# Two attention layers on one core: the values of the first block loaded early, activations in six tiles, relative terms in three

## The chip, the cores and the metric

One core of a Trainium2 chip runs the whole program. The time is device microseconds from start to end of one execution; the comparison is between medians of several executions. A profile is one further execution with the hardware profiler on; it has its own time, and a span from its first to its last instruction that is a little shorter.

Engines are named as the profile names them: PE multiplies matrices, PEld loads its stationary operand, DVE and ACT work on tensors, POOL and SP issue DMAs here (POOL nearly all stores, SP nearly all loads). In the profile SPq and POOLq are the places from which SP and POOL issue DMAs.

## The reference

Two layers of the same shape on an image of 48 x 48 tokens with 768 channels: group norm, attention with 12 heads and a relative-position term for rows and one for columns, an output projection, and the residual. Cut to what matters:

```python
h = group_norm(x, 32)                       # over tokens and 24 channels
qkv = h @ qkv_w + qkv_b                     # layer 0 adds low-rank terms to q and v
attn = einsum('bqc,bkc->bqk', q * scale, k)
rel_h = einsum('bhwc,hkc->bhwk', r_q, Rh)   # r_q is q as (head, 48, 48, 64)
rel_w = einsum('bhwc,wkc->bhwk', r_q, Rw)
attn = attn + rel_h[..., :, None] + rel_w[..., None, :]
x = x + (softmax(attn) @ v) @ proj_w + proj_b
```

In layer 1 the weights are transposed and q is scaled twice. There are 2304 queries and 2304 keys for each head, in float32.

## The kernel before

Activations lie transposed, channels on the partitions: `xT` holds six blocks of 384 tokens (NQB, QB) times six channel tiles of 128 (CT). In this version `xT` is one tile. It is filled once by transposes (`load_transposed`, L165), normalised in place (`normalise`, L246), and read by the projections.

A layer runs through these stages, PE in the order in which they stand:

1. **Projections of k and v** (`project_kv`, L474), by products of half blocks (`seven_products`, L429).
2. **Projection of q** (`project_q`, L599), in two halves of three head pairs. A half loops over the six token blocks b: three groups of q matmuls (L691), each read out by DVE (`x_q`, L697), then `store` (L616): the block is split into a high and a low part, by ACT (L384) and then DVE (L385), and both go to DRAM from POOL's queue (`f_q<-xs_q`, L626). Then ACT copies the block into `columns` (L702), and `rel_h` (L640) makes the row terms of the previous block one block late. After the sixth block comes `rel_w` (L661): 16 steps of six small matmuls each (psc, L633), each followed by a split of its result, ACT (`relw`, L387) and then DVE (L388). Only after the last step are the two parts of the column terms stored (`f_r<-relw`, L680), one DMA of 2592 KB for each part.
3. **Attention** (`attend_plain`, L852), a list of 30 blocks: for each of six head pairs, queries 0, 512, 1024, 1536 (512 each) and 2048 (256). k, v, q and the relative terms come back from DRAM scratch. In a block, 18 key tiles (NKT) of 128 keys go in batches of six: PE computes scores of six key tiles (8 matmuls q times k in two parts, and 2 matmuls that add the relative terms, L944), ACT takes the exponential, DVE sums, and then PE makes the products with v (`values`, L991) of the batch before. So PE's order is: scores 0 to 5, [values 12 to 17 of the block before], scores 6 to 11, values 0 to 5, scores 12 to 17, values 6 to 11, scores 0 to 5 of the next block, values 12 to 17. The sums of the exponentials are multiplied by ones (`denominators`, L1000, psum `ps_d`) right after values 16 (`kt == NKT - 2`), and `finish` (L1012) multiplies by the reciprocal (L1010) and stores.
4. **Output projection** (`out_project`, L1101), again by seven products of half blocks (`psy`, L1151), which loads the attention output back (`fetch_output`, L1089 and L1095) into tiles named in `first_out` (L1246) for its first pair of token blocks. In layer 0 these tiles are blocks 2 and 5 of the next layer's `xT`.

**How loads are cut.** `fetch_keys`, `fetch_queries` return a tile and a `step(g)`, g from 0 to 2; `fetched` runs step 0 of all its arguments, then step 1, then step 2. Group g of the keys is a third of the 2304 keys (768); key tiles 0 to 5 need group 0 of keys and of the relative terms, tiles 6 to 11 group 1, tiles 12 to 17 group 2. Group g of the relative terms is eight DMAs of 96 KB: rel_h (L925) and rel_w (L929) for two parts and two heads. The three groups lie in one tile `rel`. `fetch_values` issues one DMA of 1152 KB when it is called (L897), which for the first block is after all 6 loads of k, 2 of q and 24 of rel (L1026 and L1027).

**What sets the order.** A scheduler in the framework places instructions, with lists in places kept in program order (`in_order`, L158). [...] A new tile in a pool waits for every access to each whole tile whose space it takes. So one large tile comes free when its last reader is done. The program also holds a second, shifted version of attention for large inputs (`attend_plain` is the one that runs).

Of the kernel before, what the change touches and what calls it, by code (L numbers as in the profile page):

```python
# [18 lines left out]
P = 128  # L19
# [52 lines left out]
def compute(ctx: ExitStack, tc: tile.TileContext, x, layers, out, run, bad):  # L72
# [85 lines left out]
    def in_order(instruction):  # L158

        tc.keep_in_program_order(instruction)  # L160
# [4 lines left out]
    def load_transposed(xT, raw, res, weights, low_rank):  # L165


        with tc.tile_pool(name="ps_x", bufs=3, space=PSUM) as ps_x:
            loaded = [xT[:, b].rearrange("p t q -> p (t q)") for b in range(NQB)]
            loaded = [l.rearrange("p (j c) -> p j c", j=TPB) for l in loaded]  # L170
            for b in range(NQB):
                nc.sync.dma_start(loaded[b], x[ts(b, QB), :].rearrange("(j p) c -> p j c", p=P))
            weights.load(0)
            weights.begin()
            if not shifted:
                load_places()
            for b in range(NQB):
                if b == 2:
                    next(low_rank)
                for t in range(CT):  # L180
                    ps = ps_x.tile([P, QB], F32, tag="ps", name=f"psx_{b}_{t}")
                    for j in range(TPB):
                        in_order(nc.tensor.transpose(
                            ps[:, ts(j, P)], loaded[b][:, j, ts(t, P)], ident
                        ))
                    nc.scalar.copy(raw[b][:, t, :], ps)
                    nc.vector.bn_stats(stats[:, t, b, :], raw[b][:, t, :])

            weights.spread()
            for b in range(HB):  # L190
                for i in (b, b + HB):
                    in_order(nc.gpsimd.dma_start(res[i], raw[i]))

    def group_norm(xT, raw, gn, between, beside):
# [51 lines left out]
        def normalise(b):  # L246
            for t in range(CT):
                nc.vector.tensor_scalar(  # L248
                    xT[:, b, t, :], raw[b][:, t, :], mean[:, t : t + 1],
                    rstd[:, t : t + 1], ALU.subtract, ALU.mult,  # L250
                )
# [125 lines left out]
    def in_parts(hi, lo, x, scale=None, bias=None):  # L377


        if bias is not None:  # L380
            nc.scalar.activation(hi, x, AF.Identity, bias=bias)
            nc.vector.scalar_tensor_tensor(lo, x, bias, hi.bitcast(F32), ALU.add, ALU.subtract)
        elif scale is not None:
            nc.scalar.mul(hi, x, scale)  # L384
            nc.vector.scalar_tensor_tensor(lo, x, scale, hi.bitcast(F32), ALU.mult, ALU.subtract)  # L385
        else:
            nc.scalar.copy(hi, x)  # L387
            nc.vector.tensor_sub(lo, x, hi.bitcast(F32))  # L388
# [85 lines left out]
    def project_kv(ly, li, xT, kv, weights, first, normalise, PARTS, PART, kd, vd):  # L474


        with ExitStack() as es:
# [7 lines left out]
            def x_factors(b):  # L485
                for i in (b, b + HB):
                    normalise(i)
                blocks = {
                    f"{i + 1}{j + 1}": xT[:, b + j * HB, i * HP : (i + 1) * HP]
                    for i in range(2) for j in range(2)  # L490
                }
                t = kv.tile([P, 4, HP, QB], F32, tag=f"t{b}", name=f"xt_{b}")
                factors.append(sums_of_b(blocks, t))
# [105 lines left out]
    def project_q(ly, li, xT, weights, qd, rel_d):  # L599
# [4 lines left out]
        with ExitStack() as es:  # L604
# [55 lines left out]

            def rel_w(half, x):  # L661

# [3 lines left out]
                ]  # L666
                for l0 in range(0, HG, 3):
                    ps = ps_rel.tile(
                        [2 * HG, 3, HP, HG], F32, tag="rel", name=f"psc_{half}_{l0}"
# [12 lines left out]
            for half in range(2):  # L682
                w, _ = weights.take("q", half)
                columns = one.tile([P, HP, HG, HG], F32, tag="columns", name=f"columns_{half}")
                for b in range(NQB):
                    x = bp.tile([P, HP, QB], F32, tag="x", name=f"x_q_{half}_{b}")
                    for pr in range(HP):
                        pair = half * HP + pr
                        ps = ps_mm.tile([P, QB], F32, tag="mm", name=f"ps_q_{pair}_{b}")
                        for t in range(CT):  # L690
                            nc.tensor.matmul(  # L691
                                ps, lhsT=w[:, t, ts(pr, P)], rhs=xT[:, b, t, :],
                                start=(t == 0), stop=(t == CT - 1),
                            )
# [5 lines left out]
                        )  # L700
                    store(qd[half], b, x, f"xs_q_{half}_{b}", HD**-0.5)
                    nc.scalar.copy(  # L702
# [6 lines left out]
                while later:  # L709
                    later.pop()()  # L710
                rel_w(half, columns)

# [139 lines left out]
    def attend_plain(li, qd, kd, vd, rel_d, od, beside):  # L852
# [11 lines left out]
        with ExitStack() as es:  # L864
# [30 lines left out]
            def fetch_values(pair):  # L895
                v = sets[pair % 2].tile([P, NKT, P], F32, tag="v", name=f"v{li}_{pair}")
                nc.sync.dma_start(v, vd[:, ts(pair, P)].rearrange("(t p) d -> p t d", p=P))  # L897
                return v

            def fetch_queries(i, pair, at, n):  # L900
# [3 lines left out]
                into = sets[i % 2]  # L904
                rel = into.tile([P, NG, NG, QS], F32R, tag="rel", name=f"rel_{pair}_{at}")
                rel = rel[:, :, :, 0:n]
                q = [
                    into.tile([P, QS], F32R, tag=f"q{i}", name=f"q_{pair}_{at}_{i}")[:, 0:n]
                    for i in range(2)
                ]  # L910

                def step(g):
# [3 lines left out]
                    for i in range(2):  # L916
                        for r in range(2):
# [7 lines left out]
                            nc.sync.dma_start(  # L925
                                rel[row : row + KG, g].bitcast(F32),
                                rel_h[:, g : g + 1].to_broadcast((KG, NG, n)),
                            )
                            nc.sync.dma_start(  # L929
                                rel[row + KG : row + 2 * KG, g].bitcast(F32), rel_w  # L930
                            )
# [14 lines left out]
            class Block:  # L946


                def __init__(self, pair, at, n, keys, v, queries):
                    self.pair, self.at, self.n = pair, at, n  # L950
                    self.keys, self.v, self.queries = keys, v, queries
                    self.ps = self.sum = self.sums = self.first = self.rec = None

                def scores(self, kt):
# [5 lines left out]
                    steps = [(k, q) for k in keys for q in (hi, lo)]  # L960
                    steps.append((places[:, b % 2], rel[:, b // 2, c]))
                    for i, (k, q) in enumerate(steps):
# [62 lines left out]

            keys, queries = fetched(fetch_keys(0), fetch_queries(0, *blocks[0]))  # L1026
            v = fetch_values(0)  # L1027
            behind = []

            def catch_up():  # L1030

                for block, kt, pt in behind:
                    block.values(kt, pt)
                    if kt == NKT - 2:
                        block.denominators()
# [4 lines left out]
            for i, (pair, at, n) in enumerate(blocks):  # L1040
# [7 lines left out]
                if pair + 1 < CT and at == 2 * QS:  # L1048
                    next_v = fetch_values(pair + 1)
                for k0 in range(0, NKT, BATCH):  # L1050
# [50 lines left out]
    def out_project(ly, li, od, w, bt, first, res, xT, next_res, beside):  # L1101
# [3 lines left out]
        with ExitStack() as es:  # L1105
# [11 lines left out]
            for at, b in enumerate((1, 0, 2)):  # L1117
# [3 lines left out]
                if not last:  # L1121
                    y = [xT[:, i] for i in pair]
                elif at == 0:
# [60 lines left out]
    def begin(li, es):  # L1184
# [6 lines left out]
        weights.room(es)  # L1191
        xT = xp.tile([P, NQB, CT, QB], F32, tag="xT", name=f"xT{li}")
        return xT, gn, weights
# [3 lines left out]
    for li, ly in enumerate(layers):  # L1197
        last = li == len(layers) - 1
        with tc.tile_pool(name="p1_kv", bufs=1, **REUSE) as kv:
            raw = [xT[:, b] for b in range(NQB)]  # L1200
            low_rank = weights.low_rank(kv)
# [17 lines left out]
        with tc.tile_pool(name="p3_w", bufs=1, **REUSE) as p3:  # L1219
# [24 lines left out]
            else:  # L1244
                xT, gn, weights = begin(1, es)
                first_out = [xT[:, HB - 1], xT[:, NQB - 1]]  # L1246
                weights.begin()
# [72 lines left out]
```

## Time and profile before

| what | value |
|---|---|
| median of 3 runs | 3375.26 us (3374.58 to 3379.72) |
| profiled execution | 3375.62 us |
| its span | 3373.9 us |
| granted TensorE clock, mean | 0.985 |
| PE busy | 3263.2 us, 97% of the span |
| DVE busy | 2104.7 us, 62% |
| ACT busy | 1426.5 us, 42% |
| POOL busy | 387.3 us, 11% |
| DMA | 405.60 MB, mean 120 GB/s |

The profiled execution lies 0.4 us from the median, so that the working on its span can be set against the median as it is. The clock is the share of full speed that the throttle granted to TensorE. A row such as "x24 | 17.11 <-DMA v<-f_v" in the answers means 24 instructions merged, and in brackets the idle time of the engine just before, with what ended it. The positions of the stages, in us from the span's start: the q matmuls of layer 0 end at 483.3 and its attention runs from 504.0 to 1563.8; the same for layer 1 is 2129.9, and 2151.5 to 3215.9. The output projection of layer 0 begins at 1568.05.

### The profile page before, as it was taken

The numbers are of one execution on the slowest core, as the hardware profiler recorded it, in microseconds if no ns is written. First come the engines' busy times: TensorE is split into PE (matmuls) and PEld (weight loads), VectorE is DVE, ScalarE is ACT, GpSimd is POOL, SyncE is SP. The second block draws the span as 40 slices with busy tenths as digits, with TensorE's granted clock in tenths as the row PEclk, the third lists the DMA queues.
The fourth block names the chain that finished last, engine by engine and source line by source line (L and its number), as shares of the span: only waits on it lengthen the run. The fifth ranks groups of instructions, "written<-read, shape, count | busy, mean of one in ns | idle before, by whom it ended". The sixth has DMA issues, their size and how long they took to land. (4 is left out here: it accounts for less than half of the span.)

```text
span 3373.9 us, 50053 instructions
## 1 busy us (share of the span) xinstructions
PE 3263.2 (97%) x19708; PEld 2003.5 (59%) x19708; DVE 2104.7 (62%) x2275; ACT 1426.5 (42%) x1655; POOL 387.3 (11%) x719
## 2 busy tenths in 40 slices
PE   8999997999999999999989999799999999999997
PEld 5556664565666565655555566556565656665654
DVE  8432445777777677676774234477777777777753
ACT  3101444555555555553011024455555555555511
POOL 2144110000000000000012531000000000000000
PEclk9999998999999999999999999899999999999999
DMA  6333468453536353524234345753444453534241
GB/s 260 135 76 90 150 217 217 91 115 86 126 73 140 73 136 76 109 63 166 87 133 136 57 126 187 234 156 88 118 95 118 90 123 81 128 73 97 75 153 58
DMA packets 221202, 405.60 MB, mean 120 GB/s; under 512 B 41584, under 2 KB 109072, under 8 KB 217120
## 3 DMA queue, kind: packets, MB, share of 16 engines
q1 hardware_dynamic: 178656, 253.00, 30.6%
q0 software_dynamic: 42304, 149.31, 13.9%
q8 instruction: 159, 2.61, 0.3%
q14 instruction: 83, 0.68, 0.1%
HBM read 253.27 MB, written 148.89 MB: 119 GB/s over the span
## 5 line engine op out<-in xcount | busy, mean ns | idle before, releaser
L976 DVE TENSOR_TENSOR sum<-sum,pt 128x1024 f32<-128x1024 f32 (+1 forms) x960 | 1072.8, 1117 | 346.8 <-ACT pt L970 262.5
L970 ACT ACTIVATE pt<-ps_sc 128x1024 f32<-128x1024 f32 (+1 forms) x1080 | 992.0, 940 | 688.2 <-PE ps_sc L944 628.6
L944 PE MATMUL ps_sc<-q,k 64*128 64x512 f32 (+1 forms) x8640 | 1094.4, 372 | 9.5 <-ACT pt L970 8.1
L944 PEld LDWEIGHTS ps_sc<-q,k 64*128 64x128 f32 x8640 | 773.0, 185 | 272.7 <-issue 92.2
L944 PE MATMUL ps_ov<-pt,v 128*64 128x512 f32 (+1 forms) x4320 | 889.3, 556 | 31.5 <-DMA v<-f_v 31.5
L944 PEld LDWEIGHTS ps_ov<-pt,v 128*64 128x64 f32 x4320 | 294.7, 137 | 509.9 <-issue 439.4
L944 PE MATMUL ps_sc<-rel,places 64*128 64x512 f32 (+1 forms) x2160 | 409.9, 370 | 0.0
L1021 POOL DMA_DIRECT2D f_rec<-rec x120 | 58.5, 492 | 1993.3 <-DVE rec L1010 1993.1
L691 PE MATMUL ps_q<-xT,w_q 128*128 128x384 f32 x864 | 285.0, 489 | 0.7 <-DVE v L583 0.7
L1010 DVE RECIPROCAL rec<-ps_d 128x512 f32<-128x512 f32 (+1 forms) x60 | 182.2, 3037 | 100.4 <-PE ps_d L944 100.4
L691 PEld LDWEIGHTS ps_q<-xT,w_q 128*128 128x128 f32 x864 | 163.3, 191 | 110.8 <-issue 2.6
L944 PEld LDWEIGHTS ps_sc<-rel,places 64*128 64x128 f32 x2160 | 209.7, 185 | 28.8
L597 POOL DMA_DIRECT2D f_v<-v x288 | 137.9, 488 | 105.3 <-DVE v L583 94.0
L697 DVE TENSOR_SCALAR x_q<-ps_q,bt 128x384 f32<-128x384 f32 x72 | 44.4, 617 | 168.4 <-PE ps_q L691 168.4
L519 PE MATMUL ps_k<-xt,w_k 128*128 128x384 f32 x432 | 143.4, 487 | 3.6 <-DVE xt L423 2.6
L519 PE MATMUL ps_k<-xT,w_k 128*128 128x384 f32 x324 | 115.9, 511 | 4.7 <-DVE xT L248 4.6
L519 PEld LDWEIGHTS ps_k<-xt,w_k 128*128 128x128 f32 x432 | 81.5, 190 | 63.0 <-PE ps_k L519 3.0
L985 ACT CAST sum<-sum 128x1024 bf16<-128x1024 f32 (+1 forms) x60 | 57.6, 960 | 132.2 <-DVE sum L976 132.2
L384 ACT ACTIVATE xs_q<-x_q 128x1152 fp32r<-128x1152 f32 x24 | 27.9, 1163 | 196.6 <-DVE x_q L697 192.2
L988 DVE TENSOR_TENSOR sum<-sum,sum 128x1024 bf16<-128x1024 f32 (+1 forms) x60 | 67.1, 1119 | 61.6 <-ACT sum L987 61.6
L986 DVE TENSOR_TENSOR sum<-sum,sum 128x1024 f32<-128x1024 f32 (+1 forms) x60 | 67.1, 1119 | 61.6 <-ACT sum L985 61.6
L976 DVE TENSOR_TENSOR sum<-pt 128x1024 f32<-128x1024 f32 (+1 forms) x60 | 67.1, 1118 | 46.9 <-ACT pt L970 45.8
(186 smaller groups left out, 2426.0 us busy)
## 6 DMA issues: line engine op xcount, KB each, us to landing
rel<-f_r SPq DMA_DIRECT2D x1152, 96.0 KB, 4.1
f_k<-xs POOLq DMA_DIRECT2D x72, 384.0 KB, 2.9
f_q<-xs_q POOLq DMA_DIRECT2D x48, 576.0 KB, 3.8
k<-f_k SPq DMA_DIRECT2D x72, 384.0 KB, 5.5
q<-f_q SPq DMA_DIRECT2D x96, 256.0 KB, 3.0
f_r<-relh POOLq DMA_DIRECT2D x48, 432.0 KB, 5.0
f_r<-relw POOLq DMA_DIRECT2D x8, 2592.0 KB, 19.4
f_v<-v POOLq DMA_DIRECT2D x288, 48.0 KB, 2.0
```

The costliest lines, as they stand in the source:

```text
L519: nc.tensor.matmul(ps, lhsT=x, rhs=y, start=(t == 0), stop=(t == HP - 1))
L597: nc.gpsimd.dma_start(vd[to : to + KG, :], v[ts(r, KG), k])
L691: nc.tensor.matmul(ps, lhsT=w[:, t, ts(pr, P)], rhs=xT[:, b, t, :], start=(t == 0), stop=(t == CT - 1),)
L697: nc.vector.tensor_scalar(x[:, pr], ps, weights.bt[:, pair : pair + 1], ly.q_scale, ALU.add, ALU.mult,)
L944: in_order(nc.tensor.matmul(*args, **kwargs))
L970: nc.scalar.activation(pt, ps[:, :, 0 : self.n], AF.Exp)
L976: nc.vector.tensor_add(self.sum, self.first if kt == 1 else self.sum, pt)
L985: nc.scalar.copy(hi, self.sum)
L986: nc.vector.tensor_sub(self.sum, self.sum, hi)
L988: nc.vector.tensor_sub(lo, self.sum, mid)
L1010: nc.vector.reciprocal(self.rec, ps)
L1021: nc.gpsimd.dma_start(recs[li][2 * self.pair + r : 2 * self.pair + r + 1, to], self.rec[r * HD : r * HD + 1, :],)
```

## The change

Five edits, and what follows from them:

1. `xT` becomes six tiles, `xT[b]`, each with its own space and its own last reader. All uses are renamed.
2. `rel` becomes three tiles, `rel[g]`, allocated after the two q tiles.
3. `fetch_values` returns a tile and a `step`, with its one load in step 0. For the first block the tiles are allocated in the order keys, values, queries, and loaded in the order keys, queries, values: so v's load stands behind group 0 of k, q and rel, and ahead of group 1. With the new order of allocation v takes space of `x` instead of the weights' tables. For later pairs v is still asked for at query 1024.
4. In `project_q` the split and store of q of the last block of each half (`keep`) moves from before the columns copy into `rel_w`, after eight of its 16 steps. The two instructions of a scaled split are kept in program order.
5. In the last block of each layer (pair 5, queries 2048) `denominators` comes after values 17 instead of after values 16.

```diff
-            loaded = [xT[:, b].rearrange("p t q -> p (t q)") for b in range(NQB)]
+            loaded = [xT[b].rearrange("p t q -> p (t q)") for b in range(NQB)]
...
-            nc.scalar.mul(hi, x, scale)
-            nc.vector.scalar_tensor_tensor(lo, x, scale, hi.bitcast(F32), ALU.mult, ALU.subtract)
+            in_order(nc.scalar.mul(hi, x, scale))
+            in_order(nc.vector.scalar_tensor_tensor(
+                lo, x, scale, hi.bitcast(F32), ALU.mult, ALU.subtract
+            ))
...
-            def rel_w(half, x):
+            def rel_w(half, x, between):
...
                 for l0 in range(0, HG, 3):
+                    if l0 == HG // 2:
+                        between()
...
-                    store(qd[half], b, x, f"xs_q_{half}_{b}", HD**-0.5)
+                    def keep():
+                        store(qd[half], b, x, f"xs_q_{half}_{b}", HD**-0.5)
+
+                    if b < NQB - 1:
+                        keep()
...
-                rel_w(half, columns)
+                rel_w(half, columns, keep)
...
                 v = sets[pair % 2].tile([P, NKT, P], F32, tag="v", name=f"v{li}_{pair}")
-                nc.sync.dma_start(v, vd[:, ts(pair, P)].rearrange("(t p) d -> p t d", p=P))
-                return v
+
+                def step(g):
+                    if g == 0:
+                        nc.sync.dma_start(v, vd[:, ts(pair, P)].rearrange("(t p) d -> p t d", p=P))
+
+                return v, step
...
-                rel = into.tile([P, NG, NG, QS], F32R, tag="rel", name=f"rel_{pair}_{at}")
-                rel = rel[:, :, :, 0:n]
...
+                rel = [
+                    into.tile([P, NG, QS], F32R, tag=f"rel{g}", name=f"rel_{pair}_{at}_{g}")
+                    for g in range(NG)
+                ]
+                rel = [r[:, :, 0:n] for r in rel]
...
-            keys, queries = fetched(fetch_keys(0), fetch_queries(0, *blocks[0]))
-            v = fetch_values(0)
+            wanted = [fetch_keys(0), fetch_values(0), fetch_queries(0, *blocks[0])]
+            keys, queries, v = fetched(wanted[0], wanted[2], wanted[1])
...
-                    if kt == NKT - 2:
+                    if kt == NKT - (1 if block.last else 2):
                         block.denominators()
...
-        xT = xp.tile([P, NQB, CT, QB], F32, tag="xT", name=f"xT{li}")
+        xT = [
+            xp.tile([P, CT, QB], F32, tag=f"x{b}", name=f"xT{li}_{b}") for b in range(NQB)
+        ]
...
-                first_out = [xT[:, HB - 1], xT[:, NQB - 1]]
+                first_out = [xT[HB - 1], xT[NQB - 1]]
```

**Order and waits of the built programs.** Set beside each other, they show where tiles and queues end up. Before, the first k load of attention waits for the last q matmul in both layers. After, the two parts of k and of q wait for q matmuls of single blocks: in layer 0 of blocks 2, 3, 4 and 5, in layer 1 of blocks 1 to 4. The eight rel loads of group 0 and v follow with no wait of their own. Rel of group 1 waits for the last `x_q` readout of DVE. Rel of group 2 waits in layer 0 for the last psc matmul of `rel_w` (its tile lies over that stage's table), in layer 1 only for the last `x_q` readout. In both versions a load on SP also waits for the landing of the load eight before it, and the second block's q waits for the landing of the second `f_r<-relw` store. At the end of layer 0, the load of token block 2 of the output waits in the changed kernel for scores of the last block but one (query 1536), and that of block 5 for the store of that block; before, all of them wait for the last block's own PE and DVE work. In the last layer, the first of the two `judged<-f_rec` loads (L1072, a test for the shifted version) stands earlier on SP and its two DVE instructions (L1076, L1077) earlier on DVE. In half 0 of q, three q matmuls move from the head of `rel_w` into the gap behind its first step.

## What the change should do to the time

> **What bounds the kernel now.** First the page: PE is busy 97% of the span, so the time can only fall where PE waits, or where it runs slowly. Second, the waits of PE, longest in total first (us in total, times, longest):
>
> ```profile
> PE ps_ov L944 <- DMA v<-f_v: 31.5, 2, 17.1
> PE psx L183 <- DMA xT<-in_x_dram: 9.6, 5, 6.3
> PE ps_sc L944 <- ACT pt L970: 8.1, 36, 0.2
> PE psc L633 <- DVE relw L388: 5.8, 19, 0.5
> PE psc L633 <- DVE relh L388: 5.6, 4, 2.2
> ...
> PE psy L1151 <- DMA xT<-f_o: 4.3, 1, 4.3
> ...
> PE ps_d L944 <- ACT sum L985: 2.5, 1, 2.5
> ```
>
> The first line is two stalls, one for each layer, at the first use of v; the change is aimed at them, at the wait of psy, and at those of ps_d. Third, PE's order of time at the three places (start, us, what, idle before):
>
> ```profile
> 535.28 6.90 PE L944 MATMUL ps_ov<-pt,v 128*64 128x512 f32 x24 [17.11 <-DMA v<-f_v]
> 542.11 1.19 PE L944 MATMUL ps_sc<-q,k 64*128 64x512 f32 x8
> ...
> 2180.95 8.37 PE L944 MATMUL ps_ov<-pt,v 128*64 128x512 f32 x24 [14.37 <-DMA v<-f_v]
> 2189.25 1.19 PE L944 MATMUL ps_sc<-q,k 64*128 64x512 f32 x8
> ```
> ```profile
> 1568.05 6.38 PE L1151 MATMUL psy<-xT,wproj 128*128 128x384 f32 x12 [4.27 <-DMA xT<-f_o]
> ```
>
> 24 matmuls with v take 5.30 us elsewhere in the trace; here 6.90 and 8.37, since the clock had dropped during the idle time. Fourth, why v is so late. The loads of SP and stores of POOL, in order of time (start, us, what):
>
> ```profile
> 504.27 0.43 SPq L929 DMA_DIRECT2D rel<-f_r  x1
> 504.75 0.42 SPq L925 DMA_DIRECT2D rel<-f_r  x1
> 506.77 0.30 SPq L929 DMA_DIRECT2D rel<-f_r  x1
> 507.25 2.44 SPq L897 DMA_DIRECT2D v<-f_v  x1
> ```
> ```profile
> 505.43 0.52 POOL L680 DMA_DIRECT2D f_r<-relw  x1 [15.26 <-ACT relw L387]
> 506.46 0.51 POOL L680 DMA_DIRECT2D f_r<-relw  x1 [0.50 <-DVE relw L388]
> ```
>
> Both column-term stores come just before v. They end at 521.6 and 530.6, v at 535.2: 28.0 us for 1152 KB, where the ten later v loads take 6.4 to 7.6. The windows view of 511 to 518 has the DMA engines 100% busy at 330 GB/s. The rel load issued at 504.75 landed at 508.5, the next, issued at 506.77, at 522.8: **whatever is issued later than about 505 gets caught by the stores.** Layer 1 repeats it: stores issued at 2152.9 and 2153.9, ended at 2176.6; v issued at 2153.5, landed at 2180.9.
>
> **v earlier, x and rel in tiles: layer 1.** By the waits of the changed program the q loads go out at about 2118 (before: 2130), then eight rel loads and v with no wait, k and rel of group 1, and rel of group 2 once the last `x_q` is read out (2130.6). At the 0.47 us between issues seen in the trace, even 2 x 8 rel loads and four k loads behind 2130.6 are out by 2141, some 12 us ahead of the stores. So v has landed, nothing else of the first block is caught, and PE goes from the last scores (2166.6) straight into values. Gain: the wait 14.37, and 8.37 - 5.30 = 3.07 of slow clock, **17.4 us**. Late next: the second block's q, still behind the landing of the second store. PE asks for it after 6 scores and 2 batches of values more, 2166.6 + 5.3 + 6.9 + 5.3 = 2184.1; the stores end at 2176.6, and its q and eight rel loads take some 4 us: 2181, cover of 3 us.
>
> **Layer 0.** v goes out at about 488 behind rel group 0, lands by 496, and costs the loads behind it some 4 us of DMA time, which they have. But rel of group 2 has a new wait: the last psc matmul, ended at 504.1. Behind it on SP stand only the second block's loads, which wait for the stores anyway. Its eight loads go out at 504.2 to 507.5, and the stores at 505.4 and 506.5; so three to five of the eight are caught. The stall moves from v to rel: PE wants group 2 after scores 0 to 11 (ended 518.2), values 0 to 5 (5.3) and the q times k matmuls of key tile 12 (0.9), at 524.4. When do the caught loads land? Row first: one caught load of 96 KB took 16.05 us, until 522.8, and v's first packets ended at 524.5. [...] In this trace a packet of the stores is 27,648 B and takes 1.1 to 1.5 us, 24 for each engine; one of a rel load is 2 KB, four for each engine and load. [...] If the queues shared by bytes, four loads of 96 KB at half of 330 GB/s would need 2.4 us, and land by 511: no stall, gain 17.11 + 1.60 = 18.7. [...] I take the end of the stores, 530.6, and about 1.4 us for what is left: 532. Stall 532 - 524.4 = 7.6, and the slow clock behind it: the trace lost 1.60 and 3.07 us in the two restarts, [...] I take 2.4. Left: 10.0 of 18.7, **gain 8.7** (ends: 6, if the landing is at 534 with 3.1 for the clock, and 18.7).
>
> **End of layer 0.** PE ends attention at 1563.78 and waits until 1568.05. The three loads were issued at 1561.45 to 1562.57, behind the last block's own work. With blocks in tiles of their own, the loads of token blocks 2 and 5 wait for scores of query block 1536 and for its store, which landed at 1554.54; so they land near 1560.5. Gain 4.27, plus 6.38 - 4.03 = 2.35 for the clock (4.03 is what twelve such matmuls take later), 6.6; the DVE additions for the fourth product then end at 1569.7 where PE wants them at 1569.9, so I take **6.4** (ends 4.3 and 6.6).
>
> **Denominators last.** In layer 1 ps_d waited 2.51 + 1.07 + 0.43 us because DVE's sums stood behind a 3.75 us wait for a small load. Four value matmuls of 0.27 us go ahead of them: the chain of sums still ends the block, so 4.0 becomes about 3.4, and DVE's reciprocal and what follows start no later. **Gain 0.6**. In layer 0 PE waited nothing there: 0. The load of L1072 moved ahead of the output's loads costs nothing: PE has other products until its result is used.
>
> **Split of the last q block moved, twice a layer.** The columns copy (ACT) starts 1.16 us earlier, and DVE's relh split 1.36 us earlier, so the first psc matmul, which waits 2.17 us for relh, starts about 1.2 sooner. In the middle of `rel_w`, ACT's 1.16 and DVE's 1.36 come on top; there a step costs 0.97 us and DVE's split 0.924 of it, so DVE has no slack and PE waits about 1.3 longer. The two stores of 576 KB wait 10 us longer on POOL's queue, ahead of nothing but the relw stores; nobody reads them soon. In half 0 three q matmuls (about 1 us) now fill the gap behind the first step. Four times -1.2 + 1.3, and about 0.6 a layer for the fill: **gain 0.8** in all. Ends: a loss of 5.4 (4 x 1.36, nothing made up at the head), a gain of 2.5. Nearer the gain, since ACT and DVE work is the same in total.
>
> **Sum** on the profiled execution: 3375.6 - 17.4 - 8.7 - 6.4 - 0.6 - 0.8 = 3341.7. The median stands 0.4 below: **3341 us**.
>
> **The rivals.** (a) *Rel of group 2 slips through* in layer 0: loads issued by 505 did land in 4 us. Against it: the single caught load. Then 10 us more: 3331. (b) *More is caught.* The moved q stores, or SP running late, push k or rel of group 1 and 2 behind the stores in layer 1 too. For it: SP stood still for 1 to 3 us in front of several loads here. Layer 0 gains 3, layer 1 ten: 3375.6 - 3 - 10 - 7.8 = 3355. (c) *Slower: the wait is traded for a longer one.* Place: rel of group 2 at key tile 12. PE has then done as much work as before at 542 + 0.9 (layer 0) and 2190 (layer 1), so it decides when rel lands later than that in both. Each us beyond counts twice, and beyond the end of the stores (530.6, 2176.6) something would have to hold the DMA queues 12 us more, such as the q stores pushing the relw stores back. Landing 6 us beyond in both, with the 5.4 of a longer `rel_w`, less 6.4: 3375.6 + 12 + 5.4 - 6.4 = 3387. Against it: q stores need about 3 us at the 400 GB/s seen. (d) *Tiles do not free space earlier than the one tile did*, so v is still last: only the small parts, -1 to -8: 3371. Against it: the waits of the built program.
>
> **How the numbers follow.** The forecast 0.64, its own range 3334 to 3349 (layer 0 between 6 and 13, boundary 4.3 to 6.6, q split from -2.5 to +3). (a) 0.14, (b) 0.15, (c) 0.03, (d) 0.04. A range of 3331 to 3353 takes in (a) and most of what lies between the forecast and (b). Under 0.2% (6.75 us) this measurement can't tell from no change: (d) falls partly there. Faster 0.94, within 0.03, slower 0.03.
>
> **What would show it.** The line "ps_ov <- DMA v" gone from PE's waits; in layer 0 a new one, ps_sc (its rel matmul, key tile 12) for rel, 5 to 9 us, ended near 532; none in layer 1, next scores at 17 us less than before; psy behind ps_ov with no idle and 4.03 us for twelve. Rel loads of group 2 in layer 0 landing by 512 would prove (a); a wait for rel in layer 1 (b). psc's waits up by over 3 us would make the q split a loss.

## The result and the profile after

The changed kernel takes **3339.4 us** (median of 4 runs, 3338.02 to 3341.29) against 3376.15 us of the kernel before in the same comparison: a ratio of **0.989, 95% interval 0.9873 to 0.9907**. The profiled execution took 3338.02 us, its span is 3336.3 us, and the mean granted clock rose from 0.985 to 0.990.

The waits of PE in the changed kernel (us in total, times, longest), those that answer to the ones shown before:

```profile
PE psc L635 <- DVE relw L390: 8.2, 18, 1.2
...
PE ps_sc L960 <- DMA rel<-f_r: 4.8, 1, 4.8
...
PE ps_d L960 <- ACT sum L1002: 2.4, 1, 2.4
PE psc L635 <- DVE relh L390: 2.4, 4, 1.0
```

The 31.5 us for v and the 4.3 us for the output are gone. One new line stands in for them, 4.8 us for rel; psc waits 3.2 us less for relh and 2.4 us more for relw. PE's order of time at the same places, layer 0 first (start, us, what, idle before):

```profile
518.39 5.37 PE L960 MATMUL ps_ov<-pt,v 128*64 128x512 f32 x24
523.70 1.19 PE L960 MATMUL ps_sc<-q,k 64*128 64x512 f32 x8
524.73 0.38 PE L960 MATMUL ps_sc<-rel,places 64*128 64x512 f32 x1
529.94 0.76 PE L960 MATMUL ps_sc<-rel,places 64*128 64x512 f32 x1 [4.83 <-DMA rel<-f_r]
529.95 2.47 PE L960 MATMUL ps_sc<-q,k 64*128 64x512 f32 x8
...
2145.52 5.37 PE L960 MATMUL ps_ov<-pt,v 128*64 128x512 f32 x24
2150.82 1.19 PE L960 MATMUL ps_sc<-q,k 64*128 64x512 f32 x8
```
```profile
1551.40 0.50 PE L960 MATMUL ps_d<-sum,ones_k 128*64 128x256 bf16 x6
1551.83 4.14 PE L1170 MATMUL psy<-xT,wproj 128*128 128x384 f32 x12
```

In layer 0 the wait has moved to the second relative-term matmul of key tile 12 (529.94), and the matmuls behind it start slowly: eight of q times k took 2.47 us instead of 1.19, and the granted clock was 0.50 from 529.9 to 533.0. In the kernel before it was 0.50 from 525 to 535, in the first wait for v, and from 2174 to 2184, in the second and behind it, and 0.76 and 0.78 in the 7 us after each of these. In layer 1 values follow the scores, and the next scores follow the values, with nothing between. At the end of layer 0 psy stands right behind ps_d, at a clock of 1.00, where the kernel before had 0.64 over its first 6.4 us of psy. SP's queue in layer 0, then POOL's (start, us, what), show which rel loads were caught:

```profile
506.12 0.42 SPq L941 DMA_DIRECT2D rel<-f_r  x1
506.59 1.11 SPq L945 DMA_DIRECT2D rel<-f_r  x1
508.57 1.61 SPq L941 DMA_DIRECT2D rel<-f_r  x1
510.22 2.06 SPq L945 DMA_DIRECT2D rel<-f_r  x1
```
```profile
505.59 0.53 POOL L684 DMA_DIRECT2D f_r<-relw  x1 [5.89 <-ACT relw L389]
506.64 0.52 POOL L684 DMA_DIRECT2D f_r<-relw  x1 [0.52 <-DVE relw L390]
```

These are the last four of the eight rel loads of group 2; by the landing times in the trace they took 12.7, 18.0, 21.0 and 19.6 us and ended at 518.8 to 529.85. The four before them, issued at 504.33 to 505.65, took 5.2 to 6.0. The stores ended at 520.1 and 529.25.

Where the time went, by stretches between the starts of named PE instructions in the two traces (attention of layer 0 is taken to the end of its last value matmul):

| stretch | before, us | after, us | difference |
|---|---|---|---|
| start to the last psr group of layer 0 | 484.05 | 484.49 | +0.4 |
| from there to the first score | 19.96 | 19.71 | -0.25 |
| first score to the 37th value matmul (key tile 9 of the first block), layer 0 | 47.8 | 36.0 | **-11.8** |
| rest of attention, layer 0 | 1011.95 | 1011.4 | -0.6 |
| to the 19th psy matmul of layer 0 | 12.4 | 6.2 | **-6.25** |
| to the last psr group of layer 1 | 554.4 | 553.1 | -1.3 |
| from there to the first score | 20.9 | 19.6 | -1.25 |
| first score to the 37th value matmul, layer 1 | 47.5 | 30.0 | **-17.4** |
| rest of attention, layer 1 | 1016.8 | 1016.3 | -0.5 |
| to the 19th psy matmul of layer 1 | 6.9 | 8.4 | +1.5 |
| to the end | 151.2 | 151.05 | -0.1 |

The differences add up to the 37.6 us between the two spans.

### The profile page after: what moved, and what is told of

Same layout as the page of the kernel before. It is cut to its first block, busy times and chain, and to the rows that moved or that the text cites. A ratio compares the mean times of both kernels' runs of the same rounds, so it can differ in the third digit from the quotient of the medians.

```text
span 3336.3 us, 50056 instructions
## 1 busy us (share of the span) xinstructions
PE 3258.2 (98%) x19708; PEld 2002.1 (60%) x19708; DVE 2103.0 (63%) x2275; ACT 1422.4 (43%) x1655; POOL 382.8 (11%) x719
## 4 chain that ended last, share of the span: by engine, by line
PE 85%; issue 7%; ACT 2%; DVE 2%; DMA 2%; POOL 1%; SPq 1%; POOLq 0%; ACTq 0%; DVEq 0%
PE ps_sc L960 33%; PE ps_ov L960 25%; PE ps_q L695 8%; PE ps_v L521 7%; PE ps_k L521 4%; PE psy L1170 4%; ACT pt L987 1%; PE psr L635 1%; PE ps_d L960 1%; DMA rel<-f_r 1%; PE psc L635 1%; POOL f_k L565 1%; DVE relw L390 0%; ACT relw L389 0%; POOL out_dram L1200 0%
```

## The experiments

Twelve kernels ran, each beside runs of the kernel before, and each was profiled once. The first stretch of the table, in which the kernels hardly differ, ran from 482.0 to 488.1 us over all profiled runs, which is more than some of the effects looked for. So each experiment is read by its stretches, against the kernel before, and the median only says whether the sum agrees. The measured times:

| kernel | median, us | ratio to before, 95% interval |
|---|---|---|
| v_last | 3353.88 | 0.9929 (0.9912 to 0.9945) |
| one_x | 3357.68 | 0.9939 (0.9923 to 0.9956) |
| relw3 | 3324.65 | 0.9842 (0.9825 to 0.9858) |
| v_late | 3334.24 | 0.9871 (0.9854 to 0.9887) |
| keep_back | 3343.37 | 0.9902 (0.9885 to 0.9918) |
| den_back | 3339.46 | 0.9886 (0.9870 to 0.9903) |
| one_rel | 3367.65 | 0.9966 (0.9955 to 0.9978) |
| before_relw3 | 3363.64 | 0.9963 (0.9952 to 0.9975) |
| after_again | 3340.17 | 0.9889 (0.9873 to 0.9904) |
| v_late_relw3 | 3319.79 | 0.9831 (0.9818 to 0.9844) |
| relw3_half0 | 3339.13 | 0.9887 (0.9872 to 0.9902) |
| v_naive | 3374.15 | 0.9992 (0.9986 to 0.9999) |

and the three stretches that the change is about, as differences from the kernel before in us:

| kernel | first block, layer 0 | end of layer 0 | first block, layer 1 |
|---|---|---|---|
| changed kernel, two profiles | -11.8, -9.5 | -6.25, -6.25 | -17.4, -17.4 |
| v_last | -0.2 | -6.25 | -17.4 |
| one_x | -8.9 | +1.3 | -10.5 |
| one_rel | +10.6 | -6.25 | -9.5 |
| v_naive | +5.7 | +0.4 | -8.4 |
| v_late | -18.1 | -6.25 | -17.4 |
| relw3 | -18.7 | -6.25 | -17.5 |
| v_late_relw3 | -17.9 | -6.25 | -17.5 |
| relw3_half0 | -8.8 | -6.25 | -17.4 |
| before_relw3 | -0.9 | +0.2 | +0.4 |
| keep_back | -10.7 | -6.2 | -17.4 |
| den_back | -11.9 | -6.6 | -17.4 |

### Is it v's place, or the tiles? (v_last, one_x, one_rel, v_naive)

v_last keeps the tiles and gives v its old place, behind all other loads:

```diff
-                    if g == 0:
+                    if g == NG - 1:
                         nc.sync.dma_start(v, vd[:, ts(pair, P)].rearrange("(t p) d -> p t d", p=P))
```

> The changed kernel, but v of the first block is loaded in step 2, behind all of k and rel, with the six x tiles and three rel tiles kept. Theory (v's place in the queue and the early release of x work together): in layer 0 v is issued behind rel of group 2, at about 508, is caught by the column-term stores and lands at about 534; PE waits 15 to 16 us for v instead of 4.8 for rel. In layer 1 the whole list of loads still starts early, v goes out at about 2127, five us ahead of the stores, and lands by 2135: no wait, or under 1 us. Time 3339.4 + 11 = about 3350. Rival (v's place in the queue alone removed both stalls): layer 1 gets its wait of 14 us and the slow clock back too, about 3367.

PE's waits and its order of time in that kernel:

```profile
PE ps_ov L960 <- DMA v<-f_v: 15.4, 1, 15.4
```
```profile
537.50 1.12 PE L960 MATMUL ps_ov<-pt,v 128*64 128x512 f32 x2 [15.37 <-DMA v<-f_v]
...
2161.73 5.37 PE L960 MATMUL ps_ov<-pt,v 128*64 128x512 f32 x24
```

One wait for v, in layer 0, and none in layer 1: the theory. In layer 1 v was issued at 2140.3 and landed at 2149.1, a microsecond after the stores were issued at 2148.1. So in layer 1 the early start of the whole list, which the six tiles of x allow, would have been enough, with a microsecond to spare, and in layer 0 v's place is needed beside the tiles.

one_x puts x back into one tile and keeps the rest:

```diff
-        xT = [
-            xp.tile([P, CT, QB], F32, tag=f"x{b}", name=f"xT{li}_{b}") for b in range(NQB)
-        ]
+        whole = xp.tile([P, NQB, CT, QB], F32, tag="xT", name=f"xT{li}")
+        xT = [whole[:, b] for b in range(NQB)]
```

> The changed kernel with xT in one tile again, all else kept. Theory (the split of x does two things): the output loads at the end of layer 0 wait for the last block again, psy waits 4.3 us and runs its first twelve matmuls at half clock, 6.5 us; and in layer 1 the first load of k goes out 13 us later, behind the last q matmul, so that rel of group 2 is issued at about 2131 to 2136, half of it caught by the stores: a new wait for rel of 4 to 7 us in layer 1; layer 0 within 2 us of the changed kernel. Time about 3353. Rival (for attention the split of x is of no use, v's place alone does it): only the 6.5 us, about 3346.

In its order of time PE waits at three places:

```profile
534.19 0.76 PE L960 MATMUL ps_sc<-rel,places 64*128 64x512 f32 x1 [6.09 <-issue]
...
1563.57 4.62 PE L1170 MATMUL psy<-xT,wproj 128*128 128x384 f32 x7 [5.43 <-DMA xT<-f_o]
...
2169.72 1.51 PE L960 MATMUL ps_sc<-rel,places 64*128 64x512 f32 x2 [3.61 <-issue]
```

The first and the third are rel of group 2 ("issue" says only that the profile found no event for the wait; the last rel loads landed just then, in layer 1 at 2169.6 to 2170.3). In layer 1 the last four rel loads, issued at 2147.8 to 2154.2 behind stores issued at 2146.0 and 2147.0, took 16 to 20 us. So the split of x is worth 7.6 us at the end of layer 0 and 7 in layer 1. In layer 0's first block the -8.9 lies within what kernels with the tiles showed (-8.8 to -11.9), so no gain is shown there. The rival, that only the end of layer 0 needs it, falls.

one_rel keeps one tile for rel:

```diff
-                rel = [
-                    into.tile([P, NG, QS], F32R, tag=f"rel{g}", name=f"rel_{pair}_{at}_{g}")
-                    for g in range(NG)
-                ]
-                rel = [r[:, :, 0:n] for r in rel]
+                rel = into.tile([P, NG, NG, QS], F32R, tag="rel", name=f"rel_{pair}_{at}")
+                rel = [rel[:, g, :, 0:n] for g in range(NG)]
```

> The changed kernel with rel in one tile again, allocated behind q. Theory (rel needs three tiles because only its last part lies over the table read by the last psc matmul): in layer 0 all 24 rel loads wait for that matmul, group 0 is issued at 504.2 to 507.5 and half of it is caught by the column-term stores; PE waits about 25 us for group 0 before or in its first scores and runs at half clock behind it; layer 1 unchanged, since rel there waits only for x_q. About 3360. Rival (one tile would do): 3339.

```profile
528.54 0.76 PE L957 MATMUL ps_sc<-rel,places 64*128 64x512 f32 x1 [23.39 <-DMA rel<-f_r]
...
2179.47 0.76 PE L957 MATMUL ps_sc<-rel,places 64*128 64x512 f32 x1 [4.74 <-DMA rel<-f_r]
```

PE's order of time shows layer 0 as expected: group 0 comes at 528.5, and the block is 20 to 22 us longer than with three tiles. Layer 1 was expected unchanged and is not: all of rel waits there for the last `x_q` readout, so that the list reaches rel of group 2 at 2154 to 2167, around the stores issued at 2154.6, and PE waits 4.7 us.

v_naive is the kernel before with v's load in step 0 and nothing else:

```diff
-            keys, queries = fetched(fetch_keys(0), fetch_queries(0, *blocks[0]))
-            v = fetch_values(0)
+            keys, queries, v = fetched(fetch_keys(0), fetch_queries(0, *blocks[0]), fetch_values(0))
```

> The kernel before with v's load moved into step 0 and nothing else: x in one tile, rel in one tile, v allocated last, so that it lies over the table that the last psc matmul reads in layer 0. Theory (the split into tiles is what makes the early place pay): in layer 0 v waits for that matmul at the head of SP's queue until 504, k and rel of group 1 and 2 wait behind it and are caught; PE stops after key tile 5 until about 537 and layer 0 is 7 to 10 us slower than before; in layer 1 v waits only for x_q, and 13 to 17 us are gained. Together 3376 + 9 - 15 = about 3370. Rival (v's place alone does it): 3340.

```profile
529.72 1.22 PE L948 MATMUL ps_sc<-q,k 64*128 64x512 f32 x4 [15.24 <-DMA k<-f_k]
535.37 1.22 PE L948 MATMUL ps_sc<-q,k 64*128 64x512 f32 x4 [4.43 <-DMA k<-f_k]
...
2189.07 1.18 PE L948 MATMUL ps_sc<-rel,places 64*128 64x512 f32 x2 [6.43 <-DMA rel<-f_r]
```
```profile
507.45 0.38 SPq L900 DMA_DIRECT2D v<-f_v  x1
507.88 2.85 SPq L888 DMA_DIRECT2D k<-f_k  x2
```

In its SP queue v stands still until 507.45, the last psc matmul, and k of group 1 goes out behind it, into the stores. In PE's order of time the wait for v has become one for k: layer 0 is 5.7 us slower, layer 1 8.4 faster (13 to 17 had been expected; rel of group 2 got caught there), and the whole is 3 us faster than before, 0.08%. **The move of the load alone is worth nearly nothing; it pays with the tiles and the new order of allocation.** That order without the tiles was not tried.

### What is left in layer 0, and what passes beside the stores (relw3, v_late, before_relw3, v_late_relw3, after_again)

relw3 cuts each column-term store into three:

```diff
                 for found, part in zip(rel_d[1][half], parts):
-                    nc.gpsimd.dma_start(found, part.bitcast(F32))
+                    for t in range(HP):
+                        nc.gpsimd.dma_start(found[:, t], part[:, t].bitcast(F32))
```

> The changed kernel with each column-term store cut into three DMAs, one for each head pair, so that a row of 9,216 B takes the place of one of 27,648 B; same bytes. Theory [...]: rel of group 2 in layer 0 lands by 518 instead of 529.9, the wait of 4.8 us and the half clock behind it go, about 3333. Rival (the loads wait for the bytes of the stores, whatever the packets): landing stays at 527 or later, no change, 3339.

v_late has v in three tiles, the last two allocated and loaded behind rel of group 2, so that rel no longer lies over the table:

```diff
+                def third(g):
+                    return sets[pair % 2].tile(
+                        [P, BATCH, P], F32, tag=f"v{g}", name=f"v{li}_{pair}_{g}"
+                    )
+
+                v = [third(0)]
+                found = vd[:, ts(pair, P)].rearrange("(g t p) d -> g p t d", g=NG, p=P)
...
+                    elif g == NG - 1:
+                        for i in range(1, NG):
+                            v.append(third(i))
+                            nc.sync.dma_start(v[i], found[i])
...
-                            self.ps[ts(r, HD), :], lhsT=self.v[:, kt, ts(r, HD)],
+                            self.ps[ts(r, HD), :], lhsT=self.v[kt // BATCH][:, kt % BATCH, ts(r, HD)],
```

> The changed kernel with v in three tiles of six key tiles; the first is loaded as in the changed kernel, the second and third are allocated and loaded behind rel of group 2, so that they, not rel, lie over the table that the last psc matmul reads. Theory (the stall left in layer 0 is the wait of rel of group 2 for that matmul): rel of group 2 goes out before 504 and lands by 507; parts 1 and 2 of v go out at 504.3 and 504.8, the first is needed only at about 530.4 and the second at 543; no wait, about 3333. Rival (what is asked for late gets caught, and only its name changes): v's second part lands at 530 or later and the third at about 534, a wait of up to 3 us, 3336 to 3340.

Both remove the wait. In PE's order of time, first relw3 and then v_late, values follow each other at the distance of 12.41 us that one batch of values and one of scores take, with no idle time:

```profile
520.47 5.37 PE L961 MATMUL ps_ov<-pt,v 128*64 128x512 f32 x24
...
532.88 1.51 PE L961 MATMUL ps_ov<-pt,v 128*64 128x512 f32 x6
```
```profile
522.35 5.37 PE L970 MATMUL ps_ov<-pt,v 128*64 128x512 f32 x24
...
534.76 1.51 PE L970 MATMUL ps_ov<-pt,v 128*64 128x512 f32 x6
```

In relw3 the last rel load landed at 524.3, later than the 518 of the author's estimate and some 2 us before PE asked for it. In v_late the two parts of v were caught instead, landing at 529.8 and 535.5: just where the rival put them, but they are needed only at 534.8 and 547, so that nobody waits. The first gave more than its stall: 10 us of it lie in the last stretch, behind the last result (see the last section).

The same cut in the kernel before:

> The kernel before with its column-term stores cut into three DMAs each, nothing else. Theory [...]: v has 144 packets for each DMA engine against 72 of the stores instead of 24[...]; it lands some 2 us after the stores' end instead of 4.6; both stalls shrink by 2 to 3 us. The last DRAIN of POOL (10.3 us in all kernels with 687 POOL DMAs, 0.8 in the one with 703) is short here too, as the number of DMAs is 703: 10 us less. Together 3376 - 5 - 12 = about 3359 to 3361. Rival 1 (short packets alone, without the early v, remove the stalls): 3331. Rival 2 (the short DRAIN has to do with the early v): 3371.

```profile
531.68 1.98 PE L945 MATMUL ps_ov<-pt,v 128*64 128x512 f32 x4 [15.59 <-DMA v<-f_v]
...
2179.24 1.97 PE L945 MATMUL ps_ov<-pt,v 128*64 128x512 f32 x4 [15.03 <-DMA v<-f_v]
```

PE's order of time still has both waits for v, 30.6 us in total against 31.5. The expected count of 72 store packets for each DMA engine was wrong: the trace has 576 of them (9,216 B each), 36 for each of 16 engines, against 144 of v. By the packets in the trace, v's 512 B packets only began at 510.7, behind the last rel load. From 513 to 519, 239 of them passed against 242 packets of the store queue (206 of 9,216 B and 36 of a few bytes): nearly the same number, but the 239 carried 0.12 MB and the store queue's 1.90 MB. The 239 are about a tenth of v's 2304 packets, where a whole rel load has 48. This fits the cut's removing the stall for rel and hardly touching that for v; a v load in larger packets was not tried.

Both edits together, beside the changed kernel once more:

> The changed kernel with v in three tiles, the last two behind rel of group 2, and the column-term stores cut in three. Theory (both edits remove the same 6 us stall, and the cut also shortens POOL's last DRAIN by 10 us because there are 703 POOL DMAs): no more than the cut alone gave, 3323 to 3326, 0.995 of the changed kernel. Rival (the two add up, since each also shortens something else): 3319 or less.

> The changed kernel once more, unchanged, beside the other three, so that they are compared on the same chip: 3338 to 3342, with the wait of 4 to 6 us for rel of group 2 in layer 0 and none in layer 1.

The pair has the lowest median of this study: **3319.79 us** against 3340.17 of the changed kernel beside it, ratios to before of 0.9831 (0.9818 to 0.9844) and 0.9889 (0.9873 to 0.9904). Its first block in layer 0 is 17.9 us shorter than before, as with each edit alone, so the two don't add up there. Its median lies 4.9 us below relw3's, but in the profiles the difference lies in two stretches that the added edit does not touch: the first is 3.3 us shorter, and the one up to the last psr group of layer 1 2.7. So it is not shown to be faster than relw3. The second profile of the changed kernel has waits of 0.83 and 5.34 us for rel of group 2 where the first had 4.83. The same four loads were caught; measured from the first score, the last of them landed 1.5 us later, behind stores that took 1.5 us longer, and the half clock lasted 6.8 us instead of 3.4. So the first block of layer 0 varies by 2 to 3 us from run to run.

### The two small edits (keep_back, den_back)

keep_back splits and stores the last q block at its old place:

```diff
-                    if b < NQB - 1:
-                        keep()
+                    keep()
...
-                rel_w(half, columns, keep)
+                rel_w(half, columns, lambda: None)
```

> The changed kernel with the split and store of the last q block of each half back at its old place, ahead of the columns copy. Theory (moving it starts rel_w earlier by more than it costs in its middle): from the last psr to the first score, 19.7 us (layer 0) and 19.6 (layer 1) in the changed kernel, goes back to 20.0 and 20.9, psc waits 2.2 us for relh again; with the first half of each layer some 2 us slower, about 3341 to 3342. Rival (DVE has no slack in rel_w, so that the move costs as much as it gains): those stretches unchanged within 0.3 us, 3339.

Its waits of PE for the splits are those of the kernel before:

```profile
PE psc L635 <- DVE relh L390: 5.6, 4, 2.2
PE psc L635 <- DVE relw L390: 4.9, 16, 0.5
```

From the last psr group to the first score it took 19.85 us in layer 0 and 20.89 in layer 1, where the changed kernel took 19.71 and 19.63. The first halves, from the first q matmul to the last psr group, took 185.5 and 177.9 against 184.45 and 176.9. Together the move is worth 0.15 + 1.26 + 1.0 + 1.05 = **3.5 us**, and the medians agree (3343.37 against 3339.4 and 3340.17), though their intervals overlap. The other profiles agree too: from the last psr group to the first score all ten with the moved split took 19.6 to 19.8 us in both layers, all four with the old place 19.85 to 19.96 and 20.84 to 20.89. Why layer 1 gains more than layer 0 in the second half, the windows view of keep_back and then of the changed kernel shows (busy us of PE, PEld, DVE, ACT, POOL, then the granted clock, the DMA share and GB/s):

```profile
2114.40:2119.60 5.20, 3.04 (x23) 2.79 (x24) 2.84 (x4) 4.36 (x5) 1.98 (x3) 1.00 1.07 346
2119.60:2123.00 3.40, 3.40 (x16) 3.40 (x15) 1.84 (x2) 2.19 (x3) 0.73 (x2) 0.50 1.05 275
```
```profile
2110.90:2114.10 3.20, 2.18 (x16) 1.93 (x16) 0.64 (x2) 3.20 (x4) 0.00 (x0) 1.00 1.05 399
2114.10:2117.50 3.40, 2.95 (x22) 2.71 (x23) 2.29 (x4) 2.40 (x4) 1.26 (x2) 1.00 1.10 216
```

After the wait of 2.17 us for relh the clock is 0.50 for 3.4 us, and PE gets through 16 matmuls; after one of 1.04 us it stays at 1.00, and PE gets through 22. All four kernels of this study with the longer wait have this half-clock stretch in layer 1, and none of the ten with the shorter one.

den_back puts `denominators` of the last block back after values 16:

```diff
-                    if kt == NKT - (1 if block.last else 2):
+                    if kt == NKT - 2:
```

> The changed kernel with denominators of the last block back after values 16. Theory [...]: the end of attention in layer 1 comes 0.5 us later, but the first 18 psy matmuls take 6.9 us instead of 8.4: 1 us faster in all, 3338; end of layer 0 within 0.5 us. Rival [...]: the psy products stay at 8.4 and the kernel is 0.5 us slower.

Attention in layer 1 ended 1.26 us later than in the changed kernel and the first 18 psy matmuls took 0.6 us less, 7.8 instead of 8.4; in layer 0 the two stretches together were 0.4 us longer. That would make the edit worth about 0.7 us in layer 1. But the two stretches of layer 1 together, 1025.4 us here, ran from 1024.6 to 1025.6 in the ten profiles that keep the edit, and from 1023.6 to 1024.8 in the other three with the old order. So no gain of this edit is shown, nor the loss of my theory; the psy matmuls alone took 6.75 to 7.83 us with the old order and 8.0 to 8.8 with the new.

### Whose effect is the short tail? (relw3_half0)

```diff
-                    nc.gpsimd.dma_start(found, part.bitcast(F32))
+                    for t in range(HP if half == 0 else 1):
+                        t = t if half == 0 else slice(None)
+                        nc.gpsimd.dma_start(found[:, t], part[:, t].bitcast(F32))
```

> The changed kernel with the column-term stores cut in three in half 0 of each layer only: 695 POOL DMAs, and whole stores where the first block's loads are caught. Theory (two separate effects): the stall for rel of group 2 in layer 0 stays at 4 to 6 us, since the stores beside it are not cut; the last DRAIN of POOL depends on the number of DMAs alone and differs from 10.3 us or not, without regard to the stall. 3339, or 3329 if the DRAIN is short at 695. Rival (the cut itself, wherever it is, shortens the stall): the wait for rel under 2 us.

```profile
529.76 0.46 PE L962 MATMUL ps_sc<-rel,places 64*128 64x512 f32 x1 [4.36 <-issue]
...
532.62 0.76 PE L962 MATMUL ps_sc<-rel,places 64*128 64x512 f32 x1 [2.40 <-DMA rel<-f_r]
```

PE waited 4.4 and 2.4 us for rel of group 2 in layer 0, so the stall belongs to the stores beside it. POOL's DRAIN behind its last store stayed long, 10.36 us at 695 POOL DMAs.

## Why the prediction was right

The forecast was 3341 us, measured were 3339.4. That the two lie so close is in part luck. As gains, 33.9 us were forecast and 36.75 measured: layer 0's first block and the q split gave 3.1 and 2.7 us more than forecast, 1.5 us went the other way at the start of layer 1's projection, and the first stretch alone differs by up to 6 us between profiles. The steps, against the profiled execution:

- **v in layer 1:** 17.4 us forecast, 17.4 measured, in every kernel that kept all tiles. The mechanism was right too: nothing of the first block was caught, and the second block did not wait. Its q went out as the first store landed, at 2146.74, not the second as had been put on record, and the cover was 2.4 us (the eighth rel load landed at 2160.8, PE asked at 2163.2).
- **v in layer 0:** the wait moved to rel of group 2 at key tile 12, as forecast. "Four caught loads" were four. The size was off: the loads landed at 529.85 instead of 532, so that PE waited 4.83 us instead of 7.6; the slow clock took about 2.1 (17.11 + 1.60 - 4.83 - 11.8) where the author's estimate was 2.4. The gain was 11.8, in the second profile 9.5, instead of 8.7; over the five profiles with the same loads and stores at this place it was 8.8 to 11.9. The term at fault is the 1.4 us after the end of the stores, an estimate: the last load ended 0.6 us after the last store. Packets of both passed in the meantime, from 511 to 521 123 of the stores and 108 of rel. The two stores have 192 packets of 27,648 B, 12 for each of 16 engines and not the 24 put on record.
- **End of layer 0:** 6.4 forecast, 6.25 in that stretch. one_x shows that the tiles of x are the cause.
- **Denominators:** 0.6 forecast for layer 1. den_back gives 0.7, less than the spread between profiles, so this term is neither shown nor refuted. For layer 0 nothing was forecast; the 0.4 found there is as small.
- **The moved q split:** 0.8 forecast, 3.5 measured. The sign was right, the sum "four times -1.2 + 1.3" was wrong. At the head the first psc came 1.12 us earlier, as forecast. In the middle the cost was 0.9 us in layer 0 and none to be seen in layer 1, since the head's half-clock stretch went away there. In the first halves the filling by q matmuls hid the middle altogether, and 1.0 us was gained each time.
- **Not forecast:** the 18 psy matmuls at the start of layer 1's projection took 8.4 us instead of 6.9. v_naive, which leaves that end as it was, had 7.8, so at least part of it need not be of the change's making. The kernel before and before_relw3 have 3.4 us of half clock there, all the others 6.8; whether the new order of the denominators has a part in it is open.

The rivals: (a), rel slips through, did not happen, but relw3 and v_late show that its gain was there to be had, some 6 to 9 us. (b), more is caught, in layer 1 too, is what one_x and one_rel look like: it took the six tiles and the three tiles to avoid it. (c), the wait traded for a longer one, is what the bare move of the load does in layer 0, at another place than I put it: at key tile 6, for k. (d) is excluded by one_x.

## What to carry to other kernels

When a load is late beside a large store (28.0 us for v here, where later v loads took 6.4 to 7.6), look at when it *can* be issued before moving it in the program: the tile that it lands in, and whose last reader that space waits for, set its time, and a load that waits at the head of a queue holds those behind it (in v_naive v went out at 507.45 and k only at 507.88). Let what is needed last lie over the space that comes free last. Beside a large store, ask how many packets a load has: here, with the store's rows cut to a third, PE still waited 30.6 us of 31.5 for v, a load of 2304 packets (before_relw3), and no longer the 4.83 us for rel, in loads of 48 (relw3).

## What the runs showed of the hardware that was not expected

**POOL's DRAIN behind its last store took 10.28 us in some kernels and 0.80 in others.** In ten profiles with 687 POOL DMAs it took 10.28 us, in each of the three with 703 it took 0.80, and in the one with 695 10.36. In the changed kernel it runs from 3325.2 to 3335.4, behind the last result and with no work on another engine beside it, so 10 of relw3's 15 us against the changed kernel come from there, and so do 10 of the 14 us that before_relw3 gained over the kernel before. In relw3, as in the other two with 703, POOL stood still for 3.45 us in front of its last but one DMA instead (POOL's order of time in relw3):

```profile
3317.38 0.54 POOL L1201 DMA_DIRECT2D out_dram<-o  x1 [3.45 <-issue]
3318.19 0.54 POOL L1201 DMA_DIRECT2D out_dram<-o  x1 [0.27 <-issue]
```

The changed kernel has no such gap there (0.52 us before the last but one). What sets the length is not shown: the kernels with 703 DMAs also have more packets.

**The same wait of 2.17 us was followed by the half clock in layer 1 and not in layer 0.** In layer 1 this was so in four kernels of four (0.50 from 2135.8 to 2139.2 in the kernel before, from 2119.6 to 2123.0 in keep_back), and in layer 0 in none of them (1.00 from 483 to 504 in the kernel before), so here the length of the idle time alone did not decide it. No run moved the wait and nothing else, so the cause stays open, and with it how much of the 1.26 us that the moved split gained in layer 1 would come again elsewhere.
